# Four closing parts of layer 2 recorded one item earlier in each image's stage

## The chip, the cores and the metric

The kernel runs on one core of a Trainium2 chip. Five engines work side by side, each through its own list of instructions: PE (TensorE, matmuls and transposes), DVE (VectorE), ACT (ScalarE), POOL (GpSimd) and SP (SyncE, which only issues DMA here). The metric is the device time of one execution in microseconds (us), as a median of runs. Before the change it was 2453.5 us, in three runs from 2452.29 to 2455.21.

## The reference

The input `x` holds 4 images of 64 x 64 positions with 64 channels, all float32. Four layers follow each other:

```
# layer 0: attention over the 4096 positions, out = attn^T-weighted v, residual
energy = q @ k^T;  attn = softmax(energy);  x = gamma * (sum_m attn[m, n] v[m]) + x
# layer 1: layernorm, 1x1 conv to 256, 3x3 depthwise conv, gate, channel attention, 1x1 conv,
#          residual; then layernorm, 1x1 conv, gate, 1x1 conv, residual
# layer 2: attention of the image with itself, no weights
B, C, H, W = x.shape;  N = H * W;  xf = x.reshape(B, C, N)
scores = einsum('bci,bcj->bij', xf, xf)
attn = softmax(scores, axis=-1)
x = einsum('bcj,bij->bci', xf, attn).reshape(B, C, H, W) + x
# layer 3: attention with 32-wide projections, 1x1 conv, batch norm over all images, residual
f = softmax(theta_x @ phi_x^T);  w_y = (f @ g_x) @ w_W + w_b
x = x + gamma * (w_y - mean) * rsqrt(var + EPS) + beta
```

Layer 2 is the one that matters here. It takes the array's first three dimensions as batch, "channel" and rows, so that of one image 4096 x 4096 scores are formed. The scores are symmetric.

## The kernel before, in words

The fast path `fast_path` keeps all images in one SBUF tile `X` and goes through the work as one long list of **items**. `items` holds what each item records; `at(i, fn)` puts a function into `due[i]`, which is called right after item `i`. `run` walks through the list: it calls item `i`, gives the two background lanes `conv` (layer 1) and `misc` their turn, calls what is due after `i`, and gives the lanes another turn. PE, ACT, DVE and POOL carry out their instructions in exactly the order in which they were recorded (`manual_schedule`); only the DMA issues of SP are ordered by the framework. So the place at which a function is recorded decides its place in the queue of every engine that it uses.

The stages are: layer 0 of the four images with layer 1 between its items, then layer 2 of image 0, and then for `b` = 1, 2, 3 layer 2 of image `b` followed by layer 3 of image `b - 1`; last comes layer 3 of image 3. Layer 1 of image 3 still runs in the lane `conv` at the beginning of image 1's layer 2.

**Layer 2** (`layer2`, L1325) divides the 4096 keys and the 4096 queries into 8 blocks of 512. As the scores are symmetric, a block of exponentials is used once as it is and once turned. For `b` > 0 the table `FULL` gives 72 items: items 0 and 1 for block 7, and from then on ten items for each block h = 0 to 6, the first of which is item 2 + 10h. The first two items of a block h < 6 have nothing to turn; the other eight form two "runs" of four. One item `n` does this:

- `score(n)` (matmuls at L1391): four matmuls (64 x 64 weights, 512 columns) into one PSUM slot of 1024 columns; ACT takes the exponentials (L1396) into `e`.
- `turned(n)` (L1409): if the item belongs to a run, DVE transposes `e` in 32 x 32 squares into the tile `turned`. POOL sums up `e` (L1432).
- `products(n - 2)` (L1453): the exponentials of two items before, times `x`, accumulated over the block's items in two fixed PSUM banks. After a block's last item ACT and DVE bring the sums into `A` (L1462, L1468).
- `turned_products(run)` (L1479), two items after a run's last item, that is in items 13, 19, 23, 29, 33 and so on (for the first run in item 10): 64 matmuls into **two** PSUM slots. The matmuls alternate between them, two into the first slot and two into the second; DVE adds both to `A` (L1492, L1494).

**PSUM.** Of the eight banks of `PS`, six form three slots of 1024 columns. `new_ps` (L726) hands them out in turn, 0, 1, 2, 0 and so on, whoever asks, and whoever gets a slot waits until its last user has read it:

```
        s = turn_of["slots"][turn_of["ps"] % len(turn_of["slots"])]
        turn_of["ps"] += 1
        return PS[:, bass.ts(s, 1024)]
```

**The closing** of image `b - 1`'s layer 2 (`close2`, L1536) is a generator that is stepped five times during the layer 2 of image `b`. The first step, the totals, has 4 small matmuls (L1541), some reductions of the sums of exponentials (L1547), an addition that reads PSUM (L1553) and a reciprocal (L1555). Each of the following four parts takes one slot, writes 8 transposes of `A` into it (L1561, on PE), multiplies the slot in place by the reciprocals (L1563, DVE) and adds it to `X` in two additions (L1568, DVE), which end the use of the slot. The change is in the loop that gives the five steps their places (L1832). What comes after a part in the image's own data, `open3` (L1579), is added to the lane `misc` behind item 46.

Of the kernel before, what the change touches and what calls it, by code (L numbers as in the profile page):

```python
# [691 lines left out]
def fast_path(ctx: ExitStack, tc: tile.TileContext, a: dict, out: bass.AP, bad):  # L692
# [299 lines left out]
    def at(i, fn):  # L992
        due.setdefault(i, []).append(fn)
# [309 lines left out]
    def features2(b):  # L1303
        x = X[:, b]
        im[b].ko = ko = new_big("ko")
        kv = ko[:, 0:N].rearrange("p (a e n) -> p a e n", e=2, n=128)
        for g in range(4):
            ps = piece()
            for i in range(4):
                nc.tensor.transpose(ps[:, bass.ts(i, 128)], x[:, bass.ts(4 * g + i, 128)], ident)  # L1310
            for e, copy in enumerate((nc.vector.tensor_copy, nc.scalar.copy)):
                own, other = slice(64 * e, 64 * e + 64), slice(64 - 64 * e, 128 - 64 * e)
                copy(kv[own, bass.ts(g, 4), e, :], ps[own, :].rearrange("p (a n) -> p a n", n=128))
                nc.sync.dma_start(out=kv[other, bass.ts(g, 4), e, :], in_=kv[own, bass.ts(g, 4), e, :])
            yield 3.0
# [220 lines left out]
    def close2(b):  # L1536
        x, m = X[:, b], im[b]
        ps, tot, n = piece(), sums2[:, b, :], 4 * max(m.mirrored) + 4
        cs = m.cs.rearrange("p (j k) -> p j k", k=4)
        for k in range(4):  # L1540
            mm(ps[32 * k : 32 * k + 32, 0:n], sel4, cs[:, 0:n, k], start=True, stop=True)  # L1541
        g = 0
        while g < 8:
            k = g
            while k < 8 and m.count[k] == m.count[g]:
                k += 1
            nc.vector.tensor_reduce(  # L1547
                tot[:, 4 * g : 4 * k],
                m.zs[:, m.first[g] : m.first[g] + 4 * m.count[g] * (k - g)]
                .rearrange("p (t k) -> p t k", k=m.count[g]), AX.X, ALU.add,  # L1550
            )
            g = k
        nc.vector.tensor_add(tot[:, 0:n], ps[:, 0:n], tot[:, 0:n])  # L1553
        rz = sm.tile([128, 32], F32, tag="rz2", name="rz2")
        nc.vector.reciprocal(rz, tot)  # L1555
        yield
        for i in range(4):
            ps = new_ps()
            for j in range(8):
                c = 1024 * i + 128 * j  # L1560
                nc.tensor.transpose(ps[:, bass.ts(j, 128)], m.A[:, c : c + 128], ident)  # L1561
            blocks_ = ps.rearrange("p (j n) -> p j n", n=128)
            nc.vector.tensor_mul(  # L1563
                blocks_, blocks_, rz[:, bass.ts(i, 8)].unsqueeze(2).to_broadcast([128, 8, 128])
            )
            xs = x[:, bass.ts(i, 512)].rearrange("p (j h) -> p j h", h=H)
            for o in range(2):
                nc.vector.tensor_add(xs, ps.rearrange("p (j o h) -> p j o h", j=8, o=2)[:, :, o, :], xs)  # L1568
            yield
# [9 lines left out]
    def open3(b):  # L1579
        x, m = X[:, b], im[b]  # L1580
        m.tg = new_big("tg")
        m.th = m.tg[:, 0:1024]
        m.gx = m.tg[:, 1024:2048].rearrange("p (t d) -> p t d", d=32)
        for nb in range(2):
            ps = piece()
            for jj in range(2):
                for s in range(2):
                    k = 2 * s + jj
                    mm(
                        ps[32 * k : 32 * k + 32, :], thw[64 * s : 64 * s + 64, :],  # L1590
                        tok(x, s, 2 * nb + jj), start=True, stop=True,
                    )
            nc.vector.tensor_scalar_add(m.th[:, bass.ts(nb, 512)], ps, V("L3_conv_theta_b"))
            yield 3.0

        m.own = own = m.tg[:, 2048:3072].rearrange("p (s n) -> p s n", s=2)
        for s in range(2):
            ps = piece()
            for j in range(4):
                mm(  # L1600
                    ps[32 * j : 32 * j + 32, :], phw[64 * s : 64 * s + 64, :],
                    tok(x, s, j), start=True, stop=True,
                )
            nc.vector.tensor_scalar_add(own[:, s, :], ps, V("L3_conv_phi_b"))
            yield 3.0
        for i in range(2):
            ps = piece()
            for t in range(8):
                mm(ps[:, bass.ts(t, 64)], x[:, bass.ts(8 * i + t, 128)], gw, start=True, stop=True)
            for s in range(2):  # L1610
                nc.vector.tensor_add(
                    m.gx[:, 16 * s + 8 * i : 16 * s + 8 * i + 8, :],
                    ps.rearrange("p (t s d) -> p t s d", s=2, d=32)[:, :, s, :],
                    gb.unsqueeze(1).to_broadcast([128, 8, 32]),
                )
            yield 3.0

    def keys3(b):
        m = im[b]
        m.ph = new_big("ph")  # L1620
        keys = m.ph.rearrange("p (s n) -> p s n", s=2)
        for j in range(4):
            for k in range(4):
                nc.sync.dma_start(
                    out=keys[32 * k : 32 * k + 32, :, bass.ts(j, 512)],
                    in_=m.own[32 * j : 32 * j + 32, :, :],
                )
# [195 lines left out]
    for b in range(B):  # L1823
        misc_to[len(items)] = True
        f = len(items)
        if b == 0:
            layer2(b)
            misc_from[f + 89] = [features2(b + 1)]
        else:
            layer2(b, lambda b=b: keys3(b - 1))  # L1830
            turns = close2(b - 1)
            for i in (10, 13, 22, 32, 42) if b == 1 else (8, 12, 22, 32, 42):  # L1832
                at(f + i, lambda turns=turns: next(turns))
            misc_from[f + 46] = [open3(b - 1)]
            f = len(items)
            misc_to[f] = True
            layer3(b - 1)
            if b + 1 < B:
                turns = features2(b + 1)
                for i in (4, 7, 10, 13):  # L1840
                    between3[f + i] = 2, lambda turns=turns: next(turns)
# [175 lines left out]
@with_exitstack  # L2017
def conv_seq_kernel(ctx: ExitStack, tc: tile.TileContext, a: dict, out: bass.AP):
    nc = tc.nc
    flag = ctx.enter_context(tc.tile_pool(name="flag", bufs=1))  # L2020
    bad = flag.tile([1, 1], mybir.dt.int32, name="bad")
    fast_path(tc, a, out, bad)
    n_bad = nc.values_load(bad[0:1, 0:1], min_val=0, max_val=1 << 20)
    with tc.If(n_bad > 0):
        general_path(tc, a, out)
# [37 lines left out]
```

## Time and profile before

| quantity | us |
|---|---|
| median of three runs | 2453.5 (2452.29 to 2455.21) |
| profiled execution | 2456.51 |
| its span, first to last instruction | 2454.7 |
| PE busy | 2417.0 (98% of the span) |
| ACT busy | 1644.3 (67%) |
| DVE busy | 1479.3 (60%) |
| POOL busy | 540.9 (22%) |
| one L1561 transpose group to the next, in a layer 2 stage | 26.91 |
| L1563, one DVE product 128x1024 | 1.232 |
| L1568, one DVE addition 128x512 | 0.690 |
| L1409, one DVE transpose 128x1024 | 1.238 |

The profile comes from one execution. "Busy" is the sum of the durations of an engine's instructions. For PE the ends of matmuls are modelled, so consecutive ones overlap in the record, and gaps are better read from starts. In a timeline a line gives start, duration, engine, source line, operation, written and read tiles, and in brackets the idle time ahead and what ended it. PEld is PE's loading of weights, which overlaps PE. A matmul instruction of the program can appear as two records.

### The profile page before, as it was taken

How to read it: one execution, taken by the hardware profiler on the slowest of the kernel's cores; microseconds unless marked ns; L12 is line 12 of the kernel's file. 1: busy time of each engine (PE TensorE's matmuls, PEld its weight loads, DVE VectorE, ACT ScalarE, POOL GpSimd, SP SyncE). 2: the span in 40 equal slices, each digit the busy share in tenths (PEclk: the TensorE clock that was granted, in tenths of full speed). 3: DMA queues.
4: the chain of work that ended last, by engine and by line, in shares of the span. 5: the costliest groups of instructions: out<-in, count | busy, mean ns of one | idle time of the engine just before them, and what ended most of it. 6: DMA issues, size and time to landing. Idle time of an engine off the chain costs nothing.

```text
span 2454.7 us, 63654 instructions
## 1 busy us (share of the span) xinstructions
PE 2417.0 (98%) x27509; PEld 916.3 (37%) x27509; DVE 1479.3 (60%) x1794; ACT 1644.3 (67%) x3140; POOL 540.9 (22%) x381
## 2 busy tenths in 40 slices
PE   9999999999999999999999999999999999999998
PEld 3343453336333633343334442144431344421113
DVE  2020278227832773378656668876668866678886
ACT  4656766676666676668654459954479744579996
POOL 2000000000000000120135561255631365622110
PEclk9999999999999999999999999999999999999999
DMA  3000000000000000120630027610075300286554
GB/s 80 1 18 1 19 1 18 18 19 1 18 18 16 4 19 18 35 63 2 136 72 20 19 67 134 139 27 23 16 150 119 78 20 20 71 168 142 120 118 117
DMA packets 66373, 131.68 MB, mean 54 GB/s; under 512 B 12860, under 2 KB 34085, under 8 KB 66085
## 3 DMA queue, kind: packets, MB, share of 16 engines
q0 software_dynamic: 23024, 81.83, 16.5%
q1 hardware_dynamic: 42309, 43.85, 7.9%
q8 instruction: 218, 3.57, 0.6%
q10 hardware_dynamic: 752, 1.85, 0.2%
q14 instruction: 70, 0.57, 0.1%
HBM read 4.80 MB, written 4.19 MB: 4 GB/s over the span
## 4 chain that ended last, share of the span: by engine, by line
PE 86%; DVE 8%; ACT 4%; issue 1%; SPq 0%; DMA 0%; DVEq 0%; ACTq 0%
PE PS L1096 18%; PE PS L1122 18%; PE PS L1391 10%; PE PS L1453 10%; PE PS L1646 8%; PE PS L1707 8%; PE PS L1479 7%; DVE tg L1698 3%; PE PS L1206 2%; ACT e L1657 2%; ACT e L1396 1%; DVE X L1568 1%; PE PS L1561 1%; PE PS L1064 1%; PE PS L1171 1%
## 5 line engine op out<-in xcount | busy, mean ns | idle before, releaser
L1101 ACT ACTIVATE e<-PS 128x1024 f32<-128x1024 f32 x512 | 524.2, 1024 | 339.4 <-PE PS L1096 306.3
L1396 ACT ACTIVATE e<-PS 128x512 f32<-128x512 f32 x632 | 371.6, 596 | 342.0 <-PE PS L1391 321.1
L1096 PE MATMUL PS<-X,q 64*64 64x512 f32 x4096 | 573.9, 591 | 2.3 <-DVE X L979 1.7
L1122 PE MATMUL PS<-e,vq 64*64 64x512 f32 x4096 | 575.3, 592 | 0.0
L1657 ACT ACTIVATE e<-PS 128x512 f32<-128x512 f32 (+2 forms) x588 | 500.2, 921 | 59.0 <-PE PS L1646 38.1
L1698 DVE TENSOR_TENSOR tg<-tg,e 128x2048 f32<-128x2048 f32 x172 | 393.8, 2290 | 42.8 <-ACT e L1657 30.9
L1391 PE MATMUL PS<-ko 64*64 64x512 f32 x2528 | 335.6, 596 | 2.6 <-DVE u L1291 1.5
L1453 PE MATMUL PS<-e,X 64*64 64x512 f32 x2528 | 329.9, 590 | 2.5 <-issue 1.4
L1432 POOL TENSOR_TENSOR esum<-esum,e 128x1024 f32<-128x1024 f32 x132 | 314.0, 2379 | 59.7 <-ACT e L1396 52.4
L1241 DVE SCALAR_TENSOR_TENSOR y<-pad,vec,y 128x1024 f32<-128x1024 f32 x240 | 308.8, 1287 | 18.2 <-ACT y L1237 10.9
L1432 POOL TENSOR_TENSOR esum<-e 128x1024 f32<-128x1024 f32 x22 | 52.2, 2373 | 1206.2 <-ACT e L1396 1187.3
L1409 DVE STREAM_TRANSPOSE turned<-e 128x1024 f32<-128x1024 f32 x196 | 240.6, 1238 | 106.0 <-ACT e L1396 105.8
L1646 PE MATMUL PS<-tg,ph 32*64 32x512 f32 x4096 | 295.1, 612 | 1.7 <-ACT e L1657 0.8
L1096 PEld LDWEIGHTS PS<-X,q 64*64 64x64 f32 x4096 | 183.0, 133 | 261.8 <-issue 181.6
L1122 PEld LDWEIGHTS PS<-e,vq 64*64 64x64 f32 x4096 | 183.1, 133 | 253.8 <-issue 158.1
L1707 PE MATMUL PS<-e,tg 128*32 128x512 f32 x2048 | 272.5, 604 | 0.0
L1109 DVE TENSOR_REDUCE sums<-zs 128x1 f32<-128x4 f32 x128 | 19.6, 153 | 276.4 <-ACT e L1101 276.2
L1679 POOL DMA_DIRECT2D xn<-e x116 | 101.0, 892 | 292.3 <-ACT e L1657 206.0
L1453 PEld LDWEIGHTS PS<-e,X 64*64 64x64 f32 x2528 | 98.0, 133 | 176.3 <-issue 156.7
L1391 PEld LDWEIGHTS PS<-ko 64*64 64x64 f32 x2528 | 90.5, 132 | 169.9 <-issue 145.7
L1646 PEld LDWEIGHTS PS<-tg,ph 32*64 32x64 f32 x4096 | 63.4, 129 | 222.9 <-ACT e L1657 190.5
L1396 ACT ACTIVATION_READ_ACCUMULATOR e<-PS 128x1 f32 x632 | 127.3, 201 | 0.0
(219 smaller groups left out, 1692.4 us busy)
## 6 DMA issues: line engine op xcount, KB each, us to landing
xn<-e POOLq DMA_DIRECT2D x132, 512.0 KB, 5.4
esum<-e POOLq DMA_DIRECT2D x20, 512.0 KB, 5.5
xn<-t SPq DMA_DIRECT2D x64, 128.0 KB
ph<-tg SPq DMA_DIRECT2D x64, 128.0 KB
xn<-X SPq DMA_DIRECT2D x224, 32.0 KB
xr<-X SPq DMA_DIRECT2D x176, 32.0 KB
ko<-ko SPq DMA_DIRECT2D x32, 128.0 KB
xr<-in_x_dram SPq DMA_DIRECT2D x13, 256.0 KB
```

What stands on the lines that cost most here:

```text
L1096: mm(ps[64 * c : 64 * c + 64, bass.ts(r, 512)], m.q[rows_, 128 * t + 64 * c : 128 * t + 64 * c + 64], x[rows_, bass.ts(g, 512)], start=Tru ...
L1101: act(es[g // 2][:, bass.ts(g % 2, 1024)], ps, AF.Exp, bias=SHIFT0, accum_out=zs[:, g : g + 1],)
L1122: ins = mm(PS[64 * s : 64 * s + 64, 2048 + 512 * j : 2560 + 512 * j], vq[rows_, :], es[j // 2][rows_, k : k + 512], start=t == 0 and i < 2 ...
L1241: stt(y1, win, wt, y1, ALU.mult, ALU.add)
L1391: mm(ps[64 * c : 64 * c + 64, bass.ts(r, 512)], m.ko[rows_, k : k + 64], m.ko[rows_, bass.ts(h, 512)], start=True, stop=True,)
L1396: act(e[:, bass.ts(r, 512)], ps[:, bass.ts(r, 512)], AF.Exp, bias=SHIFT2, accum_out=slot(g, 2 * u + r),)
L1432: nc.gpsimd.tensor_add(esum, st["e"][mine_t[h][0]] if k == 1 else esum, e)
L1453: mm(st["acc"][r][64 * c : 64 * c + 64, :], xw[rows_, 4 * g + 2 * u + c, :], st["e"][n][rows_, bass.ts(c, 512)], start=n == mine[h][0], st ...
L1646: mm(PS[64 * c : 64 * c + 64, bass.ts(banks[k], 512)], m.ph[32 * k : 32 * k + 32, 128 * mc + 64 * c : 128 * mc + 64 * c + 64], m.th[32 * k ...
L1657: act(e[:, 512 * lo : 512 * k], PS[:, 512 * banks[lo] : 512 * banks[lo] + 512 * (k - lo)], AF.Exp,)
L1698: nc.vector.tensor_add(esum, esum, e)
L1707: mm(st["y"][32 * k : 32 * k + 32, :], m.gx[:, i % 32, :], es[i][:, bass.ts(k, 512)], start=mc == 0, stop=i % 32 == 31,)
```

## The change

The first step of image 1's closing goes from behind item 10 to behind item 9 of the stage, and the four parts go from behind 13, 22, 32 and 42 to behind 11, 21, 31 and 41. In the stages of images 2 and 3 the first step stays behind item 8, and the parts go from behind 12, 22, 32 and 42 to behind 11, 21, 31 and 41. Nothing else is altered; what each step does is the same.

```diff
         else:
             layer2(b, lambda b=b: keys3(b - 1))
             turns = close2(b - 1)
-            for i in (10, 13, 22, 32, 42) if b == 1 else (8, 12, 22, 32, 42):
+            for i in (9 if b == 1 else 8, 11, 21, 31, 41):
                 at(f + i, lambda turns=turns: next(turns))
             misc_from[f + 46] = [open3(b - 1)]
```

## The prediction

> **What bounds the kernel now.** I read the page first: its first part and the shares of the chain say which engine sets the end.
>
> ```profile
> PE 2417.0 (98%) x27509; PEld 916.3 (37%) x27509; DVE 1479.3 (60%) x1794; ACT 1644.3 (67%) x3140; POOL 540.9 (22%) x381
> ...
> PE 86%; DVE 8%; ACT 4%; issue 1%; SPq 0%; DMA 0%; DVEq 0%; ACTq 0%
> ```
>
> PE (TensorE) has 98% and most of the chain, so time is won only where PE stands still. Next I asked for PE's waits, from image 1's layer 2 to image 3's (1270 to 2050 us).
>
> ```profile
> PE PS L1479 <- DVE X L1568: 3.5, 11, 0.3
> ...
> PE PS L1479 <- DVE sums L1553: 0.5, 2, 0.3
> ...
> PE PS L1391 <- DVE A L1494: 0.3, 1, 0.3
> ```
>
> The columns are us in total, times, longest. The matmuls of the turned products (L1479) wait eleven times for the last addition of a closing part (L1568). There are twelve parts, four in each of three layer 2 stages. 0.32 us each looks small, but an idle time counts from the modelled end of the matmul before, so I looked at starts. This is the chain of the stage of image 2 from 1648 us; item 23's turned product is the x124 line, the next undisturbed one the x128 line.
>
> ```profile
> 1652.21 0.86 PE PS L1453 x8
> 1653.07 1.04 PE PS L1561 x8
> 1654.11 0.02 issue
> 1654.13 1.24 DVE PS L1563
> 1655.38 0.02 issue
> 1655.40 0.70 DVE X L1568
> 1656.10 0.02 issue
> 1656.12 0.70 DVE X L1568
> 1656.83 0.04 issue
> 1656.87 3.70 PE PS L1479 x124
> ...
> 1671.03 3.64 PE PS L1479 x128
> 1674.67 1.02 PE PS L1391 x8
> ```
>
> The chain leaves PE after the eight transposes (L1561), runs through DVE's product and two additions and comes back at 1656.87. PE's own list of starts shows the loss: item 23's turned product starts at 1655.90, issues 4 of its 128 records (both matmuls into the first of its two PSUM slots), stops until 1656.87, and the next score starts at 1660.50. That is 4.60 us; the undisturbed one, 1670.96 to 1674.60, takes 3.64. **The stall costs 0.96 us.** The period says the same: L1561 starts at 1626.09, 1653.00, 1679.91, 26.91 us apart. Without a stall ten items are 10 x 1.716 (two scores start at 1662.27 and 1663.98) + 2 x 3.64 + 1.03 for the transposes + 0.48 for six changes of tile shape (0.11 or 0.05 each, against 0.86) = 25.95. So 0.95 to 0.96, and all eleven are alike in the trace.
>
> Last, DVE between the same times, because the new place is right behind its transposes (L1409).
>
> ```profile
> 1650.19 1.25 DVE L1409 STREAM_TRANSPOSE turned<-e 128x1024 f32<-128x1024 f32 x1 [0.94 <-ACT e L1396]
> 1651.85 1.25 DVE L1409 STREAM_TRANSPOSE turned<-e 128x1024 f32<-128x1024 f32 x1 [0.41 <-ACT e L1396]
> 1654.13 1.23 DVE L1563 TENSOR_TENSOR PS<-PS,rz 128x1024 f32<-128x1024 f32 x1 [1.04 <-PE PS L1561]
> 1655.40 1.42 DVE L1568 TENSOR_TENSOR X<-PS,X 128x512 f32<-128x512 f32 x2
> ```
>
> Items 20 and 21 have a DVE transpose each, item 22 has none: DVE idles 1.04 us waiting for L1561 while PE will soon wait for DVE.
>
> **The Trainium skill.** "Perfetto Trace Analysis", Optimization Strategy: the same gap repeating on the engine that should be saturated can mean that there is too little PSUM for the next tile. The trace agrees: eleven equal stalls on a slot. The same page, under Tensor Engine Instruction, says that matmul ends are estimated; hence starts above. "PSUM — Partial Sum Buffer", Engine vs sequencer instructions: matmuls run in program order and VectorE is strictly FIFO; in the timeline the score behind a stalled turned product also waits. "VectorE: DVE Perf Modes", The TRN2 errata: an fp32 tensor_tensor takes (N+151)/0.96 ns, 691 for 512; L1568 takes 691.
>
> **The change, part by part.** No instruction is added or removed. A part issues 8 transposes on PE and three DVE operations; it issues no DMA and nothing on ACT, POOL or SP, so no DMA queue is passed.
>
> *Eleven parts, from behind item 12, 22, 32 or 42 to one item earlier.* On PE the eight transposes move ahead of one score and one product group (1.72 us). On DVE nothing is passed: items 12, 22, 32, 42 give it no work, so its order stays. The slots rotate over three. In the old order score 22 takes q, the part r, score 23 p, and the turned product q and r: its second slot is the part's, and it has only score 23 and product 21 (0.90 + 0.97 us) as cover. In the new order the part takes q, score 22 r, score 23 p, and the turned product again q and r, so now its *first* slot is the part's, with one more score and product as cover.
>
> New times, from the old starts. Product 19 starts at 1650.32, so the transposes at +0.97 = 1651.29; score 22 at +1.03 = 1652.32; product 20 +0.90 = 1653.22; score 23 1654.08; product 21 1654.94; turned product +0.97 = 1655.91, as before, since the same work lies before it. DVE: L1409 of item 21 stays at 1651.85; a following operation starts 1.17 to 1.25 us after a transpose (two in a row at 1668.90 take 2.36), so L1563 at 1653.02 to 1653.10, while its transposes are done at 1652.42. The additions start 1.27 later and end 1.42 after that: 1655.71 to 1655.79, and PE resumes 0.05 behind such an end: 1655.76 to 1655.84. PE wants the slot at 1655.91. **The margin is only 0.07 to 0.15 us**, but nothing is left of the stall.
>
> Other waits at the new place: slot q was last read by the additions of item 19's turned product, which end at 1649.26, 2.0 us before the transposes; score 22's slot was item 20's, whose exponentials end near 1650.1, before 1652.32; the turned product's second slot, score 22's, is free 2.31 after its start, 1654.63. For item 11 in images 2 and 3, L1409 starts at 1624.94 and the turned product at 1629.0 in the new order: the same margin (1628.8 against 1629.0). Behind a late part stand the additions L1468, needed only at product 22, 4.5 us after the turned product starts.
>
> Gain: 11 x 0.95 = **10.45 us**.
>
> *Image 1's first two steps: the totals from item 10 to 9, the first part from 13 to 11.* Here the convolution work of image 3 still runs between, and the part had no stall, as it stood behind the turned product. Totals before: score 11 starts 0.57 after L1541 with 0.28 named as a wait. Removing them behind item 10 saves (1.05 + 0.57) - 0.91 = 0.71; behind item 9 they cost 1.55 - 0.86 = 0.69. The turned product of item 10 then finds its second slot held by the totals: L1409 of item 9 at 1276.20, + 1.17 + 0.58 (five reductions) + 0.24 gives 1278.24 against a want at 1277.9 to 1278.0: a stall of 0.3. The part at item 11 costs 2.05 - 0.86 = 1.19 and saves 2.05 - 0.91 = 1.14 at its old place. Its slot comes round at score 13: want 1288.49, DVE free at 1289.04 (item 11's L1409 at 1285.13, + 1.17 + 1.27 + 1.42 + 0.05), a stall of 0.55. A small old stall of 0.22 behind it (score 15, 1296.39 to 1297.47 instead of 0.86) goes. Sum -0.71 + 0.69 + 0.3 + 1.19 - 1.14 + 0.55 - 0.22 = **+0.66 us**; the trace doesn't show this order, so 0 to 1.5.
>
> *Downstream.* In the layer 3 stretch 1800 to 1920 PE is busy 119.24 of 120 us, so PE passes the gain on; ACT with 114.18 would bind only after another 5 us of cover.
>
> **Sum.** 10.45 - 0.66 = 9.8 us. Against the profiled execution: 2456.51 (span 2454.7 and 1.8 around it) - 9.8 = 2446.7. That execution stood 3.0 above the runs' median of 2453.5, so the median becomes 2443.7, 0.4% less. The runs themselves lie from 2452.29 to 2455.21; a change under about 0.2% (4.9 us) can't be told from none.
>
> **Rivals.**
>
> *A. The margin is missed by a little* (chance 0.13). A 0.1 us margin is worked out from starts rounded to hundredths, and the held slot is now the first one, so all 64 matmuls stand behind it. If DVE is 0.2 to 0.5 us later than computed, 0.1 to 0.4 returns eleven times: gain 5 to 9, 2444.5 to 2448.5. For it: the thinness. Against it: L1409 sits 1.15 us before L1561's old start in every steady part looked at.
>
> *B. The gain is given back* (0.08). The stalls go, but later work, such as the start of layer 3 with keys from SP's queue, is fixed by something other than PE: 2450 to 2455. Against it: no DMA is named among PE's waits in the layer 2 and 3 stages. That the change doesn't do what it says belongs here; PE's order is written out by hand, so I see no way.
>
> *C. Slower* (0.04). DVE starts L1563 late because item 21's L1409 comes before it, and the turned product stops at its first matmul. It decides once DVE frees the slot 1.05 us after the time above (0.1 margin + 0.95 old stall); at 1.6 us late each stall is 1.5, and 11 x 0.55 + 0.7 = 6.8 us slower, 2460. Against it: that L1409 already has its input early, and DVE's order is unchanged.
>
> **How the numbers follow.** The forecast (stalls gone, image 1 losing 0 to 1.5) has 0.75: gains of 8.9 to 10.6 and some 1.5 us for the median of runs, 2441.4 to 2446. The range runs on through rival A to 2448.5 and leaves out B, C and a tail below. Faster by over 0.2%: forecast and nearly all of A, 0.87. Same: B and a rest of A, 0.09. Slower: C, 0.04.
>
> **What would show it.** Right: no wait of L1479 for L1568, or a trace of it; L1561 in the steady parts 25.95 us apart; L1563 starting right behind L1409 with no idle time; in image 1 new short waits of L1479 for L1553 and of L1391 for L1568. Wrong: eleven waits of L1479 for L1568 still there, now at x128 with no 4 records ahead; or a shorter layer 2 and a longer layer 3.

## The result, and the profile after

| | before | after |
|---|---|---|
| median of 7 runs, us | 2453.29 (2452.07 to 2455.21) | 2443.26 (2441.9 to 2450.08) |
| ratio, 95% interval | | 0.9962 [0.9952, 0.9972] |
| profiled execution, us (its span) | 2456.51 (2454.7) | 2444.88 (2443.1) |

The change makes the kernel 10.0 us faster by the medians. On the page of the kernel after, the first part gives the busy times, and the shares of the chain show DVE's share down (from 8% to 5%) and PE's up (from 86% to 87%):

```profile
PE 2410.9 (99%) x27509; PEld 914.5 (37%) x27509; DVE 1477.5 (60%) x1794; ACT 1642.9 (67%) x3140; POOL 541.1 (22%) x381
...
PE 87%; DVE 5%; ACT 4%; DMA 1%; issue 1%; SPq 1%; POOL 0%; ACTq 0%; DVEq 0%; POOLq 0%
```

PE's waits of the kernel after in the layer 2 stages (1270 to 2050 us; us in total, times, longest):

```profile
PE PS L1719 <- DVE tg L1698: 1.1, 2, 0.6
PE PS L1646 <- ACT e L1657: 0.5, 2, 0.3
PE PS L1479 <- DVE sums L1553: 0.5, 2, 0.3
PE PS L1391 <- DVE X L1568: 0.5, 1, 0.5
```

The eleven waits of L1479 for L1568 are gone. What is new is one wait of a score (L1391) for L1568, in image 1's stage; the two waits for L1553, in the stages of images 2 and 3, stand in the kernel before too. The chain of the kernel after from 1648 us no longer leaves PE around the closing part:

```profile
1671.31 1.02 PE PS L1561 x8
1672.34 1.02 PE PS L1391 x8
1673.35 0.86 PE PS L1453 x8
1674.21 0.86 PE PS L1391 x8
1675.07 0.86 PE PS L1453 x8
1675.93 3.64 PE PS L1479 x128
```

All 128 records of the turned product run in one piece, with one score and one product group more between them and the transposes than before. And this is DVE of the kernel after in item 21 and behind it:

```profile
1645.85 1.25 DVE L1409 STREAM_TRANSPOSE turned<-e 128x1024 f32<-128x1024 f32 x1 [0.41 <-ACT e L1396]
1647.02 1.20 DVE L1563 TENSOR_TENSOR PS<-PS,rz 128x1024 f32<-128x1024 f32 x1
1648.25 1.42 DVE L1568 TENSOR_TENSOR X<-PS,X 128x512 f32<-128x512 f32 x2
```

The 1.04 us of idle time ahead of L1563 have gone: it starts 1.17 us behind L1409, and the additions end at 1649.67. PE starts the turned product at 1649.91.

To see where the time went I compared the PE starts of the same instruction in both profiles. The lead of the kernel after grows stage by stage:

| up to here (start before / after) | lead, us | grew by |
|---|---|---|
| L1206 ahead of image 1's closing (1265.60 / 1262.74) | 2.86 | |
| past image 1's totals and first part, L1453 (1298.38 / 1296.23) | 2.15 | -0.71 |
| past image 1's other three parts, L1391 (1377.65 / 1372.63) | 5.02 | 2.87 |
| past image 2's four parts, L1453 (1776.68 / 1767.81) | 8.87 | 3.85 |
| past image 3's four parts, L1453 (2109.92 / 2097.19) | 12.73 | 3.86 |
| end of the span (2454.7 / 2443.1) | 11.6 | -1.1 |

The stages give 10.6 - 0.7 = 9.9 us. The 2.86 us at the top stand ahead of the first instruction that the change moves. Most of it arises around the end of image 0's layer 2 and in the first items of image 1's: the profiled execution of before has a gap of 1.4 us and a wait of 1.5 us there that in the one after are none and 0.4. That execution also stood 3.2 us above its median. So these are not the change's. The 1.1 us at the end lie in the last layer 3, where the chain of the kernel after passes through the landing of a DMA. What made it late there wasn't tried.

### The profile page after: what moved, and what is told of

It is laid out like the page before. It is cut to its first block, busy times and chain, and to the rows that moved or that the text cites. A ratio compares the mean times of both kernels' runs of the same rounds, so it can differ in the third digit from the quotient of the medians.

```text
span 2443.1 us, 63650 instructions
## 1 busy us (share of the span) xinstructions
PE 2410.9 (99%) x27509; PEld 914.5 (37%) x27509; DVE 1477.5 (60%) x1794; ACT 1642.9 (67%) x3140; POOL 541.1 (22%) x381
## 4 chain that ended last, share of the span: by engine, by line
PE 87%; DVE 5%; ACT 4%; DMA 1%; issue 1%; SPq 1%; POOL 0%; ACTq 0%; DVEq 0%; POOLq 0%
PE PS L1096 18%; PE PS L1122 18%; PE PS L1391 10%; PE PS L1453 10%; PE PS L1646 8%; PE PS L1707 8%; PE PS L1479 7%; PE PS L1206 2%; DVE tg L1698 2%; ACT e L1657 2%; DMA xn<-e 1%; ACT e L1396 1%; PE PS L1064 1%; PE PS L1171 1%; PE PS L1270 1%
## 5 line engine op out<-in xcount | busy, mean ns | idle before, releaser
L1391 PE MATMUL PS<-ko 64*64 64x512 f32 x2528 | 335.6, 596 | 1.7 <-ACT ko L1313 0.8
L1453 PE MATMUL PS<-e,X 64*64 64x512 f32 x2528 | 329.6, 590 | 1.1 <-ACT own L1465 1.1
L1409 DVE STREAM_TRANSPOSE turned<-e 128x1024 f32<-128x1024 f32 x196 | 240.6, 1238 | 107.5 <-ACT e L1396 107.2
L1646 PE MATMUL PS<-tg,ph 32*64 32x512 f32 x4096 | 295.7, 612 | 2.5 <-ACT e L1657 1.6
L1453 PEld LDWEIGHTS PS<-e,X 64*64 64x64 f32 x2528 | 98.0, 133 | 174.7 <-issue 155.1
L1391 PEld LDWEIGHTS PS<-ko 64*64 64x64 f32 x2528 | 90.3, 132 | 169.1 <-issue 145.1
L1646 PEld LDWEIGHTS PS<-tg,ph 32*64 32x64 f32 x4096 | 63.3, 129 | 224.4 <-ACT e L1657 192.0
```

Source lines behind the costliest of these rows:

```text
L1391: mm(ps[64 * c : 64 * c + 64, bass.ts(r, 512)], m.ko[rows_, k : k + 64], m.ko[rows_, bass.ts(h, 512)], start=True, stop=True,)
L1453: mm(st["acc"][r][64 * c : 64 * c + 64, :], xw[rows_, 4 * g + 2 * u + c, :], st["e"][n][rows_, bass.ts(c, 512)], start=n == mine[h][0], st ...
L1646: mm(PS[64 * c : 64 * c + 64, bass.ts(banks[k], 512)], m.ph[32 * k : 32 * k + 32, 128 * mc + 64 * c : 128 * mc + 64 * c + 64], m.th[32 * k ...
```

## The experiments

The theory, called cover theory in the expectations: a part costs PE whatever is left of the time until DVE's last reading of the part's PSUM slot, once the work that PE has before it wants that slot is done. The rivals: that DVE's work must simply come earlier; that any user between the scores stalls; that DVE's work itself, and not the slot, holds PE.

**Image 1's first two steps put back** (the rest as in the changed kernel).

```diff
-            for i in (9 if b == 1 else 8, 11, 21, 31, 41):
+            for i in (10, 13, 21, 31, 41) if b == 1 else (8, 11, 21, 31, 41):
```

> The changed kernel with image 1's totals and first part put back to items 10 and 13. Cover theory (a stall lasts from the moment PE wants a slot until the part's last DVE addition on it ends): the new stall of score 13 (0.45 us) and the longer turned product of item 10 (4.24 instead of 3.64 us) go, and the old short waits at scores 11 and 15 come back; the ten-item parts stay without stall. 0.7 us less than the changed kernel, about 2442.5 us against 2453.3 before, which the times can hardly show but the trace can: a score 13 without a wait on L1568. Rival (the whole change pays, image 1's first two steps too): 1 us or more above the changed kernel.

Measured: 2443.46 us against 2453.14 before, ratio 0.9964 [0.995, 0.9978]. In time it can't be told from the changed kernel. In the starts it can: its lead over the changed kernel grows from 1.64 to 2.34 us over these steps, by 0.70, and stays there through the layer 2 stages. In the profiled execution this lead is lost in the last layer 3, where PE waits 1.8 us for ACT (0.8 in the changed kernel) and then runs 3.41 us at half clock. Its PE starts show score 13 (1282.56) right behind the L1295 ahead of it, without a wait:

```profile
1281.55 1.08 PE L1295 MATMUL PS<-u,pw 128*64 128x512 f32 x4
1282.56 1.09 PE L1391 MATMUL PS<-ko 64*64 64x512 f32 x8
```

The changed kernel has it 1.53 us behind and not 1.01:

```profile
1284.67 1.08 PE L1295 MATMUL PS<-u,pw 128*64 128x512 f32 x4
1286.20 1.09 PE L1391 MATMUL PS<-ko 64*64 64x512 f32 x8 [0.45 <-DVE X L1568]
```

So image 1's first two steps are the part of the change that loses, 0.7 us.

**One item later instead of earlier.**

```diff
-            for i in (10, 13, 22, 32, 42) if b == 1 else (8, 12, 22, 32, 42):
+            for i in (10, 13, 23, 33, 43) if b == 1 else (8, 13, 23, 33, 43):
```

> The kernel before with the parts one item LATER: behind items 13, 23, 33 and 43, that is behind the turned product instead of ahead of it. Cover theory: the part's slot is wanted again only at the third slot after it, score 26, some 4.6 us behind the end of the turned product, and DVE is done with it at 4.3, so no stall: 11 x 0.95 = 10.5 us less than before, 2442.8 us. Rival (earliness: the part's DVE work must come before, so that DVE is free in time): a later part is worse or no better than before, 2453 us or more. Rival (slot count: any user between the scores makes PE wait): no gain.

Measured: 2440.41 us, ratio 0.9948 [0.9935, 0.9962], 12.7 us less. The rivals of earliness and of slot count fall: a later place does as well as an earlier one, and here a bit better by the starts. PE's starts in the stage of image 2:

```profile
1645.90 3.71 PE L1479 MATMUL PS<-turned,xn 32*64 32x256 f32 x128
1649.55 1.09 PE L1561 MATMUL PS<-ident,A 128*128 128x128 f32 x8
1650.57 1.09 PE L1391 MATMUL PS<-ko 64*64 64x512 f32 x8
```

I had expected 10.5. Each part gained 1.11 us and not 0.96 by the starts. The 0.15 more go with changes of tile shape on PE: transposes between a product group and a score cost 0.11 at their start and 0.05 behind them, on top of their own 1.03. Directly behind the turned product (3.65 us from start to start, 3.64 without them) these are paid anyway. The Trainium skill, "TensorEngine Tiling (Array Packing)", Key Properties, says that a change of tiling mode drains TensorE; the 0.05 and 0.11 us stand at such changes here. That the drain is their cause was not tested apart.

**Old places, but the slot free after one DVE operation.**

```diff
+            done = m.A[:, bass.ts(i, 1024)]
             nc.vector.tensor_mul(
-                blocks_, blocks_, rz[:, bass.ts(i, 8)].unsqueeze(2).to_broadcast([128, 8, 128])
+                done.rearrange("p (j n) -> p j n", n=128), blocks_,
+                rz[:, bass.ts(i, 8)].unsqueeze(2).to_broadcast([128, 8, 128]),
             )
...
-                nc.vector.tensor_add(xs, ps.rearrange("p (j o h) -> p j o h", j=8, o=2)[:, :, o, :], xs)
+                nc.vector.tensor_add(xs, done.rearrange("p (j o h) -> p j o h", j=8, o=2)[:, :, o, :], xs)
```

> The kernel before with its places unchanged (10, 13, 22, 32, 42 and 8, 12, 22, 32, 42). The part's product L1563 is written to the dead block of A in SBUF instead of back into PSUM, and the two additions read it there: DVE has the same three operations, but the PSUM slot is free after the first. Cover theory: the slot comes free 1.4 us earlier, at 1655.4 instead of 1656.8 on the clock of the profile before, ahead of PE's want at 1656.0: the eleven stalls go without any move, 10.5 us less, 2442.8 us. Rival (it is DVE's work or its order that holds PE, not the slot): as before, 2453.3 us.

Measured: 2440.58 us, ratio 0.9951 [0.9937, 0.9964], 12.6 us less. DVE and PE around one part in this kernel:

```profile
1646.46 1.23 DVE L1564 TENSOR_TENSOR A<-PS,rz 128x1024 f32<-128x1024 f32 x1 [1.04 <-PE PS L1561]
1647.72 2.35 DVE L1570 TENSOR_TENSOR X<-A,X 128x512 f32<-128x512 f32 x2
1648.23 3.71 PE L1479 MATMUL PS<-turned,xn 32*64 32x256 f32 x128
```

The additions (now L1570) even take longer, 2.35 us, and end at 1650.07, while the turned product starts at 1648.23 and runs through. DVE's work on the part doesn't hold PE; its hold on the slot does. The stages give 10.7 us, where 10.5 were expected. The rest I had missed: image 3's own closing, in the last layer 3, uses the same function and had a stall there too (the wait of L1646 for L1568, 0.7 us by name). Its lead grows there from 14.31 to 15.77, by 1.5 us.

**DVE made later by one addition in SBUF** (in the changed kernel).

```diff
+            spent = m.A[:, 1024 * i : 1024 * i + 256]
+            nc.vector.tensor_add(spent, spent, spent)
             nc.vector.tensor_mul(
```

> The changed kernel with one more DVE addition of 128x256 (by the duration of other fp32 additions 0.42 to 0.44 us; it doubles a dead block of A, so the output stays the reference's) ahead of each part's product. In the trace of the changed kernel the last addition ends 0.23 to 0.24 us before the turned product starts, 0.19 with the 0.05 that PE takes to resume. Cover theory: stalls of 0.25 in eleven parts and 0.44 more in image 1's first: 3.2 us above the changed kernel, about 2446.5 us. If the margin were larger than the trace says: no change, 2443.3. If the hand-over of the first slot costs more than its delay (the mode change before it is paid twice): 0.35 to 0.45 each, 4.3 to 5.4 us, 2447.6 to 2448.7.

Measured: 2474.11 us, ratio 1.0083 [1.007, 1.0097]. That is 31 us above the changed kernel where 3 were expected, since the operation didn't take 0.43 us. DVE of this kernel, and POOL at the same time:

```profile
1657.48 1.25 DVE L1409 STREAM_TRANSPOSE turned<-e 128x1024 f32<-128x1024 f32 x1 [0.41 <-ACT e L1396]
1658.64 2.37 DVE L1564 TENSOR_TENSOR A<-A 128x256 f32<-128x256 f32 x1
1660.94 1.22 DVE L1565 TENSOR_TENSOR PS<-PS,rz 128x1024 f32<-128x1024 f32 x1
```
```profile
1655.93 4.80 POOL L1432 TENSOR_TENSOR esum<-esum,e 128x1024 f32<-128x1024 f32 x2 [0.36 <-ACT e L1396]
```

It took 2.37 us and ended 0.28 behind POOL's addition (1660.73). At image 2's first part it took 1.59 and ended 0.29 behind POOL's (1632.64); in image 3's closing in layer 3, without POOL's additions, it took 0.42. The Trainium skill, "SBUF — State Buffer", Who interferes with whom, says that a DVE instruction with two SBUF inputs contends with a GpSimd instruction that reads SBUF; here it lost 1.9 us (2.37 less 0.42). What it did to PE is told in the last section.

**DVE made later by an operation on the slot** (in the changed kernel; 8 columns of `ones` in place of 2 for the longer one).

```diff
+            nc.vector.tensor_mul(
+                blocks_[:, 0:2], blocks_[:, 0:2], ones[:, 0:2].unsqueeze(2).to_broadcast([128, 2, 128])
+            )
             nc.vector.tensor_mul(
```

> The changed kernel with one more DVE product of 128x256 ahead of each part's product, now on the part's own PSUM slot and times one (same result, one SBUF input only, so that it can't be held up by POOL as the addition of two SBUF inputs in run late256 was). About 0.45 us more on DVE. Cover theory: stalls of 0.45 - 0.19 = 0.26 in eleven parts and 0.45 in image 1's first: 3.3 us above the changed kernel, 2446.6. Rival (margin larger or smaller than the trace's 0.19): 2443.3 with no stall at all, or 2448.2 and more with the whole 0.45 in each part.

> The same with 128x1024 columns, about 1.23 us more on DVE. Cover theory: stalls of 1.04 in eleven parts and 1.23 more in image 1's first, 12.7 us above the changed kernel: 2456.0 us, 2.7 us above the kernel before, since 1.23 is more than the 1.14 by which the change brought the part's end ahead. The predicted turning point was 1.05. Rival (a longer stall also slows PE's clock, as stalls of 2.1 us did in run late256): up to 1.7 more in some parts, 2461 to 2472.

Measured: 2450.43 us, ratio 0.999 [0.9983, 0.9996] for the short one; 2462.82 us, ratio 1.004 [1.0026, 1.0054] for the long one. Both lie above what was expected, 2446.6 and 2456.0, but the stalls grow with the delay and the eleven are alike. The short operation's one SBUF input is `ones`, and it took 0.40 us while POOL was adding. PE's waits of the two kernels, the short one first:

```profile
PE PS L1479 <- DVE X L1571: 3.2, 11, 0.3
...
PE PS L1649 <- DVE X L1571: 1.5, 1, 1.5
PE PS L1391 <- DVE X L1571: 1.0, 1, 1.0
```
```profile
PE PS L1479 <- DVE X L1571: 11.1, 11, 1.0
PE PS L1649 <- DVE X L1571: 2.2, 1, 2.2
PE PS L1391 <- DVE X L1571: 1.7, 1, 1.7
```

By the starts each part loses 0.365 us with the short operation and 1.09 with the long one. How far each operation delays DVE is read from the traces. This is DVE around one part with the short one, whose transposes (L1561) start at 1646.51 and whose turned product starts at 1651.49:

```profile
1648.24 0.40 DVE L1563 TENSOR_TENSOR PS<-PS,ones 128x256 f32<-128x256 f32 x1
1648.75 1.23 DVE L1566 TENSOR_TENSOR PS<-PS,rz 128x1024 f32<-128x1024 f32 x1
1650.02 1.42 DVE L1571 TENSOR_TENSOR X<-PS,X 128x512 f32<-128x512 f32 x2
```

From the start of the transposes to the end of the last addition it is 4.92 us here, 5.65 with the long operation and 4.38 in the changed kernel (1645.29 to 1649.67). So the delays are 0.54 and 1.27 us, and the margin comes out at 0.18 with both. The trace of the changed kernel says nearly the same, 0.19: 0.24 us from the end of the last addition to the start of the turned product, less the 0.05 that PE takes in these two kernels to start behind such an end. In the expectations it was the short operation's delay that was too small, not the margin that was too large: it was put at its own duration, 0.45, which came out as 0.40. But the product starts 0.51 behind its start, and the first addition 1.27 behind the product's start instead of 1.23.

Image 1's first part has no margin and loses the whole delay, 0.5 and 1.3. Image 3's closing in layer 3, which I had left out again, loses 2.6 and 6.4 by the starts right behind it; about 1.6 of each is PE at half clock (last section). With the eleven parts this gives 4.0 + 0.5 + 2.6 = 7.1 and 11.9 + 1.3 + 6.4 = 19.6 us above the changed kernel; measured are 7.2 and 19.6. The time of the long operation lies in the range of the slower clock's rival, 2461 to 2472, but none of its eleven parts shows it: each turned product takes 3.64 us behind its stall. The half clock comes in layer 3 alone.

**The short operation in the kernel before.** The edit is the same, with the old places.

> The kernel before with the same 0.45 us on DVE ahead of each part's product. At the old places there is no margin, so each of the eleven stalls grows by the whole 0.45, and image 1's score 15, which waited 0.22, by 0.45 too: 5.4 us above before, 2458.6 us. If the stall were set by PE's order alone and not by DVE's end: as before, 2453.2.

Measured: 2456.57 us, ratio 1.0012 [1.0006, 1.0019], 3.5 us above before where 5.4 were expected. By the starts most of the loss is in the last layer 3, 3.2 us, of which about 1.6 are PE at half clock; over the eleven parts the lead over the kernel before changes only from 3.98 to 2.88, 0.1 each. The reason for so little stands in this kernel's timeline:

```profile
1649.42 1.09 PE L1561 MATMUL PS<-ident,A 128*128 128x128 f32 x8
1650.11 0.43 DVE L1563 TENSOR_TENSOR PS<-PS,ones 128x256 f32<-128x256 f32 x1 [0.60 <-PE PS L1561]
1650.65 1.23 DVE L1566 TENSOR_TENSOR PS<-PS,rz 128x1024 f32<-128x1024 f32 x1
```

The added operation reads only the first 256 columns and starts 0.69 us behind the start of the transposes. It runs while the later ones are still written, so that the whole product comes only 0.1 later than it would (1.13 behind 1649.42). Other than at the new place, DVE here waits for PE. The run doesn't test what it was made for; 0.1 us of delay and 0.1 us of stall agree.

**Both remedies together**: behind items 13, 23, 33 and 43, with the product written to `A`.

> Parts behind items 13, 23, 33 and 43 and the product written to A in SBUF. In the traces of the two runs alone, the place behind the turned product gave 1.11 per part (0.96 of stall and 0.15 for one change of tile shape less), and the early slot 0.96 per part and 1.5 us in image 3's closing in layer 3. Cover theory: the stall can be won only once, so 11 x 1.11 + 1.5 = 13.7 us below before, 2439.5 us. Rival (the two add up): 24 us below, 2429.

Measured: 2439.34 us, ratio 0.9944 [0.993, 0.9957]. This is the lowest median, 13.8 us below before and 3.9 below the changed kernel; over the later place alone (2440.41) it is 1.1 us, which the ranges of the runs don't tell apart. The sum of both gains, 24 us, isn't there: a stall can be won once.

## Why the prediction was right, point by point

- **The stall of 0.96 us, eleven times**: right. The parts now start 25.95 us apart (1645.29, 1671.24, 1697.19), as worked out, and the leads grow by 0.96 per part. That the slot carries it is shown by the run with the slot freed early at the old places.
- **DVE at the new place**: right. L1563 starts 1.17 us behind L1409.
- **The margin of 0.07 to 0.15**: it was there, but a bit larger, 0.18 by the two runs that use it up. L1563 starts 1.17 us behind L1409, the lower end of what was taken, and the additions follow it by 1.23 us and not 1.27.
- **Image 1's first two steps, +0.66**: measured +0.71 (+0.70 by the run that puts them back), but two terms of this sum were off and cancelled. The totals cost less (score 10 starts 1.18 us behind product 7, not 1.55), and so the turned product of item 10 came earlier to a slot that DVE freed at the same time: it takes 4.24 us instead of 3.64, 0.6 more and not 0.3. That the sum came out is luck in these two terms. The sign named for it, a wait of L1479 for L1553 in image 1, isn't named by the profile; only the starts show it. The stall of score 13 was 0.52 (1.53 less 1.01), worked out as 0.55.
- **Downstream passes it on**: right within 1.1 us in the profiled execution. The two profiled executions leave 9.9 - 1.1 = 8.8 us to the change, the medians 10.0; worked out were 9.8.
- **Rival A** (margin missed): not so, but near; a delay of 0.54 us cost 0.365 per part. **Rival B**: not so. **Rival C** put the turning point at a delay of 1.05 us; with the margin of 0.18 it is 0.18 + 0.96 = 1.14. The long operation, a delay of 1.27, makes each stall 1.09, 0.13 above the old 0.96. That kernel is 9.7 us slower than before; by the starts 1.4 of this are the eleven parts', 2.0 image 1's first steps' and 6.4 layer 3's.
- **What I hadn't seen**: that closing from the other side of the turned product would give more than the change, and that image 3's closing in layer 3 has the same stall.

## What to carry to other kernels

Count the slots between two users of a rotating buffer and the work that covers each of them; a stall of the bounding engine can be removed by moving the user to either side or by freeing the slot sooner, and only once. Read a stall's cost from the starts and the period and not from the named idle time, which here was 0.32 of 0.96 us. The margin that is left can be read from the trace, as the gap less the time that the waiting engine takes to start (0.24 - 0.05 us here); added delays test it, if the delay itself is read from their traces and not taken from the duration of what was added.

## What the runs showed of the hardware

A longer stall cost more than its length. In the run late256 the eleven turned products wait 1.3 us (2 of them) or 2.0 to 2.07 us (9). Five of the nine then took 5.33 us from their start to the next score, not 3.64; none of the two, and none in the run with stalls of 1.0 us, did. In the trace the granted clock, the share of its full clock that TensorE gets (the column PEclk below), is at half for 3.41 us after each of the five, from 1320.14, 1350.87, 1664.89, 1722.92 and 2036.94. These starts are 9, 92, 17 and 92 times 3.413 us apart, so they lie on one grid. These are stretches of the grid around one of the five stalls (PE idle from 1661.61 to 1663.66), and around one of the four that were spared (idle from 1691.38 to 1693.44):

```profile
core 0: us, PE busy (x), PEclk, DMA share, GB/s
1661.48:1664.89 3.41, 1.35 (x52) 1.00 0.00 0
1664.89:1668.30 3.41, 3.41 (x80) 0.50 0.02 5
1668.30:1671.72 3.42, 3.42 (x59) 1.00 0.12 31
1688.79:1692.20 3.41, 2.58 (x26) 1.00 0.00 0
1692.20:1695.61 3.41, 2.17 (x80) 1.00 0.02 5
1695.61:1699.02 3.41, 3.41 (x81) 1.00 0.09 23
```

The five idle times that lie in one stretch (but for 0.04 us of one) are followed by half clock in the next stretch, and that costs 1.7 us (5.33 - 3.64). The other four are split between two stretches, with at most 1.38 us in either, and cost nothing more. So for these nine the place on the grid goes with whether 2 us of idle time are followed by another 1.7. The Trainium skill, "TensorE: Matmul & The Clock Gate", What's actually happening, speaks of a free-running window of about 3.4 us; the grid agrees with it, but an idle time of 2.0 us, less than such a window, was enough.

A shorter one can be enough too. In slot_late256 and in slot_late256_old PE waits 1.49 us in image 3's closing in layer 3 (L1649), within one stretch, and half clock follows for 3.41 us. But in slot_late1024 a wait of 1.7 us within one stretch, in image 1's stage, is not followed by it. So the length of the idle time isn't all that decides, and what else does stays open.
